# The last seven of 79 expert blocks behind a condition, and half a shared-expert batch moved to the end

## The chip, the cores and the metric

The kernel runs on one core of a Trainium2 chip. The metric is the device time of one execution in microseconds, where lower is better; a kernel's time is the median of several runs. The engines that matter here are TensorE (PE, matmuls; PEld is its weight load), VectorE (DVE), ScalarE (ACT), GpSimd (POOL) and SyncE (SP, which issues most DMAs). Each engine works through its own list of instructions in order, and waits for the others through semaphores.

## The reference: what is computed

One transformer block on four batches of 512 tokens of width 256, in fp32. A modulation from a small conditioning input scales and shifts two layer norms and gates two residuals. The first half is causal attention with 32 heads of width 8. The second half is a mixture of experts, cut here to its core:

```python
x = x + ga * attention(h)
h = layernorm(x) * (1 + cb) + sb
cw = combine_weights(h, gate_w)             # [T, 16]: four experts a token, the others 0
for e in range(16):
    a = swiglu(h @ expert_up_w[e].T)        # 256 -> 2 x 176
    out = out + cw[:, e:e+1] * (a @ expert_down_w[e].T)
out = out + swiglu(h @ shared_up_w.T) @ shared_down_w.T   # the shared expert, 2 x 352
x = x + gb * out
```

Which experts a token takes is known only at run time: of four groups of four experts the two with the greatest score are kept, and of these the four best experts.

## The kernel before, in words

**Routing.** After the attention of each batch, its normalized rows (256 values, the token's number and 16 weights) are scattered by POOL into `rows_d`, a table in HBM with a stretch of rows for each expert. VectorE counts how many rows each expert has (`upto`). `make_table` (L318) works out, from those counts, a list of blocks of 128 rows: `last` holds a running count of the blocks begun, and `row` and `of` hold, one partition a block, the first row of a block and its expert. 2048 tokens x 4 experts are 64 full blocks, and each of 16 experts may leave one begun block, so `NBLK` = 64 + 15 = 79 blocks always suffice. Blocks that are not begun read a row stretch that is blank, and add zeros to a row of the accumulator that nobody reads.

**Experts.** In `ffn` (L1501) each block `j` goes through `block(j)` (L1550): SP reads the block's row into a register and fetches x (`fetch`, L1560), TensorE transposes it (`pt`, L1571), ACT copies it (`xt`), TensorE multiplies with the expert's up weights (`pu`, L1591), ACT and VectorE form the gated product (`sg_b` L1601, `a_b` L1605), TensorE transposes it back (`pb`, L1610), VectorE copies it (`at_b`, L1614), TensorE multiplies with the down weights (`py`, L1619), ACT weighs the rows (`y_b`, L1629), and POOL scatters them with an add into an accumulator in HBM (`put`, L1632). There are two accumulators by turns, and a third from block 63 (`LAST`) on; a scatter waits until the one before it on the same accumulator has landed.

**Shared expert.** `shared(b, ...)` (L398) works on half batches of 256 tokens: three chunks of up matmuls (L417), tanh on ACT (L428), two products on VectorE (L436, L437), two outputs of down matmuls (L455), a gating on VectorE (L465) and an add into `x_sb` on POOL (L471). All eight halves are planned ahead of the blocks; the last runs between the first blocks.

**Ends.** The rows of an expert are ordered by batch, so the first batches are complete before all blocks are done. `end(b, n, due)` (L1674) loads the two accumulators' rows of batch b with SP (L1687), and adds, gates and adds the residual on VectorE (L1693, L1696, L1701), in two halves, then stores (L1704). It is planned at block n + 14, with n = 31, 47 and 63 for the first three batches. Its operations on VectorE also wait, in the plan, for the copies (`backs`) of later blocks, one each, so that they are spread over them. The fourth batch is finished after the last block (L1728 to L1739): twelve loads by SP and ACT, then adds on POOL and VectorE, and four stores.

**Order.** On TensorE, VectorE, ACT and SP the order is the kernel's own: `Plan` (L85) takes operations with a cost, needs, a due time and buffers that they take and give back, and issues at each step the one that can start first. It works with the estimates written beside the operations; once issued, an engine's order is fixed. POOL's order is left to the framework's scheduler, apart from some links.

## Time and profile before

| what | value |
|---|---|
| median of 3 runs (lowest, highest) | 724.9 us (723.86, 727.31) |
| the profiled execution's own time | 723.11 us |
| its span, first to last instruction | 721.4 us |
| mean granted TensorE clock | 0.962 |
| PE busy | 648.1 us (90%) |
| DVE, ACT, POOL busy | 441.5, 314.7, 360.3 us |
| 316 records of pu (L1591) | 106.6 us, 460 ns each |
| 316 records of py (L1619) | 81.4 us, 379 ns each |
| 79 scatters put (L1632) | 128.0 us, 1621 ns each |

Records of TensorE overlap: a matmul's record lasts longer than the distance to the next one, so time on TensorE is read from the starts. The profile tells the 40 equal slices of the span as digits, tenths of busy time. The expert blocks fill about the last third of the span.

### The profile page before, as it was taken

The page shows a single profiled execution, that of the slowest core. Times are in us where ns is not written, and L with a number is a line of the kernel's source. Part 1 is how long each engine was busy: PE and PEld are TensorE (multiplying, and loading weights), DVE is VectorE, ACT ScalarE, POOL GpSimd, SP SyncE. Part 2 cuts the span into 40 slices and gives each one's busy share as a digit, 9 for nine tenths or more (in the row PEclk, how much of TensorE's full clock was granted, in tenths as well). Part 3 has the DMA queues.
Part 4 walks back from the last instruction along what each step waited for, and adds up shares of the span by engine and source line. Part 5 has one row for each costly group of instructions (what it writes and reads, how often), then busy time and mean ns, then how long its engine had stood idle before and what let it go on. Part 6 is the DMA issues. An engine that isn't in the chain of part 4 may idle for free.

```text
span 721.4 us, 12934 instructions
## 1 busy us (share of the span) xinstructions
PE 648.1 (90%) x4188; PEld 401.3 (56%) x4188; DVE 441.5 (61%) x1206; ACT 314.7 (44%) x551; POOL 360.3 (50%) x454
## 2 busy tenths in 40 slices
PE   4778899999999999999998798799999999999980
PEld 3343344454544545445453277588777777777750
DVE  4568678889888788887977035644333334444343
ACT  1313455664556645555655511013344444444430
POOL 7401233336277453664727625552566666666682
PEclk9789999999999999999999879899999999999995
DMA  5351161212234232554201178851467678777765
GB/s 167 80 130 26 42 170 45 53 41 69 61 111 118 78 98 68 161 164 126 65 4 60 44 225 232 209 143 33 81 109 108 110 110 180 128 160 139 148 88 132
DMA packets 58002, 77.81 MB, mean 108 GB/s; under 512 B 8620, under 2 KB 50316, under 8 KB 56784
## 3 DMA queue, kind: packets, MB, share of 16 engines
q1 hardware_dynamic: 42714, 56.96, 28.6%
q0 software_dynamic: 14448, 19.31, 16.6%
q10 hardware_dynamic: 774, 0.72, 0.4%
q8 instruction: 34, 0.56, 0.3%
q14 instruction: 32, 0.26, 0.1%
HBM read 43.73 MB, written 32.83 MB: 106 GB/s over the span
## 4 chain that ended last, share of the span: by engine, by line
PE 66%; DVE 19%; DMA 5%; issue 4%; ACT 2%; POOL 2%; SPq 0%; ACTq 0%; DVEq 0%; POOLq 0%
PE pu L1591 13%; PE py L1619 10%; PE pa L1012 9%; PE pr L899 8%; DVE mx_s L920 7%; PE p L1042 7%; PE pu L417 4%; PE py L455 3%; PE pr L907 2%; PE pb L1610 2%; PE pt L1571 2%; DMA qx<-mrow 2%; ACT ex L1054 2%; DVE xn L654 2%; DMA kx<-kd 1%
## 5 line engine op out<-in xcount | busy, mean ns | idle before, releaser
L920 DVE TENSOR_REDUCE mx_s<-pr 128x1 f32<-128x384 f32 (+3 forms) x352 | 212.5, 635 | 39.3 <-PE pr L907 35.9
L1054 ACT ACTIVATE ex<-p 128x1024 f32<-128x1024 f32 (+1 forms) x192 | 162.5, 882 | 105.7 <-PE p L1042 97.6
L1061 POOL TENSOR_SCALAR_AFFINE_SELECT ex<-ex 128x256 f32<-128x256 f32 (+1 forms) x192 | 93.1, 491 | 193.8 <-ACT ex L1054 192.4
L1632 POOL DMA_INDIRECT acc_d<-y_b,token x79 | 128.0, 1621 | 77.2 <-DVE token L1584 26.3
L899 PE MATMUL pr<-kx,qx 125*128 125x384 bf16 (+3 forms) x512 | 122.8, 304 | 12.6 <-DVE mx_s L920 9.7
L1591 PE MATMUL pu<-up_sb,xt 128*128 x316 | 106.6, 460 | 0.0
L1042 PE MATMUL p<-qx,kx 128*128 128x256 bf16 (+3 forms) x512 | 97.5, 302 | 7.3 <-DMA qx<-mrow 4.4
L1012 PE MATMUL pa<-ex,vaug 128*32 128x512 f32 (+3 forms) x1024 | 96.6, 448 | 2.2 <-POOL ex L1061 2.1
L907 PE MATMUL pr<-seen,ident_h 128*128 128x128 bf16 (+2 forms) x352 | 86.7, 246 | 0.0
L899 PEld LDWEIGHTS <-qx 125*128 125x128 bf16 x512 | 46.6, 99 | 67.5 <-issue 48.7
L1619 PE MATMUL py<-down_sb,at_b 88*128 x316 | 81.4, 379 | 1.2 <-DVE at_b L1614 1.2
L1605 DVE TENSOR_TENSOR a_b<-sg_b,pu 128x176 f32<-128x176 f32 x79 | 26.6, 337 | 80.2 <-ACT sg_b L1601 80.2
L1383 POOL DMA_INDIRECT rows_d<-row,slot x64 | 62.7, 979 | 25.1 <-DVE slot L1380 12.6
L1619 PEld LDWEIGHTS py<-down_sb,at_b 88*128 88x128 f32 x316 | 59.7, 189 | 22.1 <-ACT y_b L1629 1.7
L1591 PEld LDWEIGHTS pu<-up_sb,xt 128*128 128x128 f32 x316 | 53.9, 190 | 16.8
L1042 PEld LDWEIGHTS <-kx 128*128 128x128 bf16 x512 | 41.0, 98 | 39.6 <-issue 23.7
L1629 ACT ACTIVATE y_b<-py,cw_b 128x256 f32<-128x256 f32 x79 | 37.5, 474 | 46.1 <-PE py L1619 46.1
L1614 DVE COPY at_b<-pb 88x256 f32<-88x256 f32 x79 | 33.2, 420 | 36.0 <-PE pb L1610 36.0
L1601 ACT ACTIVATE sg_b<-pu 128x176 f32<-128x176 f32 x79 | 25.1, 318 | 59.9 <-PE pu L1591 59.8
L417 PE MATMUL pu<-h2t,sup_sb 128*128 128x256 f32 (+1 forms) x192 | 47.7, 402 | 1.7 <-DVE a L437 1.7
L907 PEld LDWEIGHTS <-ident_h 128*128 128x128 bf16 x352 | 34.5, 98 | 25.7 <-issue 19.6
L1012 PEld LDWEIGHTS pa<-ex,vaug 128*32 128x32 f32 x1024 | 21.6, 108 | 36.5 <-issue 20.2
(184 smaller groups left out, 730.7 us busy)
## 6 DMA issues: line engine op xcount, KB each, us to landing
x<-rows_d SPq DMA_DIRECT2D x79, 136.5 KB
qx<-qd SPq DMA_DIRECT2D x48, 192.0 KB
up_sb<-in_up_t SPq DMA_DIRECT2D x8, 704.0 KB
acc_d<-blank SPq DMA_DIRECT2D x18, 256.0 KB
qd<-pt SPq DMA_DIRECT2D x16, 192.0 KB
s<-acc_d SPq DMA_DIRECT2D x12, 256.0 KB
down_sb<-in_down_t SPq DMA_DIRECT2D x8, 352.0 KB
rows_d<-blank SPq DMA_DIRECT2D x17, 136.5 KB
```

Of the source, the lines that this page charges most:

```text
L417: nc.tensor.matmul(st["p"][:rows, w, :], lhsT=sup_sb[:, k, c0 : c0 + rows], rhs=h2t[:, k, c1 : c1 + half], start=(k == 0), stop=(k == KC - 1),
L899: nc.tensor.matmul(pr[:, h, :], lhsT=qx[s % 3][:QKZ, REP * j + r + h, ts(i, P)], rhs=kx[s % 3][:QKZ, j, :w], start=True, stop=False, skip_ ...
L907: nc.tensor.matmul(pr[:, :, w - P :], lhsT=ident_h, rhs=seen.unsqueeze(1).to_broadcast([P, n, P]), start=False, stop=True, skip_group_chec ...
L920: nc.vector.tensor_reduce(mx[s][:, i, c0 : c0 + n], st["pr"], AX.X, ALU.max)
L1012: nc.tensor.matmul(st["pa"][32 * r : 32 * r + 32, c * P :], lhsT=vaugs[b % 2][:, c, SLOTS * n + j, :], rhs=exs[r], start=(j == 0 and c == ...
L1042: nc.tensor.matmul(pe[:, h, :], lhsT=kx[s % 3][:, j, ts(c, P)], rhs=qx[s % 3][:, REP * j + r + h, c * P :], start=True, stop=True,)
L1054: nc.scalar.activation(ex, st["pe"], AF.Exp, scale=qk_scale)
L1061: nc.gpsimd.affine_select(out=st["ex"][:, :, 0:P], in_=st["ex"][:, :, 0:P], pattern=[[0, n], [1, P]], base=0, channel_multiplier=-1, compa ...
L1383: dma = nc.gpsimd.indirect_dma_start(out=rows_d, out_offset=bass.IndirectOffsetOnAxis(ap=st["slot"][:, i, k : k + 1], axis=0), in_=st["row ...
L1591: nc.tensor.matmul(st["pu"], lhsT=st["xt"][:, k, :], rhs=up_sb[:, bass.ds(st["e"], 1), k, :].rearrange("p e f -> p (e f)"), start=(k == 0) ...
L1619: nc.tensor.matmul(st["py"], lhsT=st["at"][:, c, :], rhs=down_sb[:, bass.ds(st["e"], 1), c, :].rearrange("p e d -> p (e d)"), start=(c == ...
L1632: dma = nc.gpsimd.indirect_dma_start(out=acc_d[j % (2 if j < LAST else 3)], out_offset=bass.IndirectOffsetOnAxis(ap=st["token"][:, 0:1], a ...
```

## The change

A constant `SURE` = 72 splits the blocks. Blocks 0 to 71 are issued as before. The table also gives the number of blocks begun, as an integer. After the 72 blocks, every engine loads that number into a register, and blocks 72 to 78 stand in a part that runs only if it is over 72. What follows the conditional part is the end of the fourth batch, as before.

The second half of the last batch's shared expert is no longer planned ahead of the blocks. It is planned after block 71, with a late due time, and may start only once the up matmuls of block 71 are issued.

The end of the third batch is planned at block 71 in place of block 77, since no later block is sure. The list of copies that its VectorE operations wait for is filled up with None, which stands for no wait.

```diff
+SURE = 72
...
         def rows():
...
+            last = t["last"]
...
-            for name in ("row", "of"):
+            t["all"] = last[:, B * E - 1 :]
+            for name in ("row", "of", "all"):
                 t[f"{name}_i"] = pool.tile([P, 1], mybir.dt.int32, name=f"{name}_i", bufs=1)
                 nc.vector.tensor_copy(t[f"{name}_i"], t[name])
...
-    def shared(b, due, up_bank, down_bank, first=None):
+    def shared(b, due, up_bank, down_bank, first=None, halves=(0, 1)):
...
-        for n in range(2):
+        for n in halves:
             unit(n)
...
-            shared(b, due, up_bank, down_bank)
+            shared(b, due, up_bank, down_bank, halves=(0, 1) if b < B - 1 else (0,))
...
                 "PE", 1.28, up, [xt, weights], due, takes=[h["pu"]], gives=[h["xt"]]
             )
+            ups.append(u)
...
-        backs = []
+        backs, ups = [], []
...
-            pace = iter(backs[n + 8 :])
+            pace = iter(backs[n + 8 :] + [None] * 6)
...
-        for j in range(NBLK):
+        for j in range(SURE):
             puts.append(block(j))
             for b in range(B - 1):
                 n = (b + 1) * S * TOPK // P + E - 1
-                if j == n + 14:
+                if j == min(n + 14, SURE - 1):
                     end(b, n, 300.0 + n)
+        shared(B - 1, lambda: 1000.0, up_bank, down_bank, ups[-1], halves=(1,))
         plan.go()
+        many = nc.values_load(
+            t["all_i"][0:1, 0:1], min_val=0, max_val=NBLK,
+            skip_runtime_bounds_check_because="counted above",
+        )
+        with tc.If(many > SURE):
+            for j in range(SURE, NBLK):
+                puts.append(block(j))
+            plan.go()
```

## The prediction

> **What bounds the kernel now.** I read the page first, then the chain that ended last, then the busy time by stretches, then the engines' timelines where the change lands.
>
> The page, its span line and three of its rows of 40 slices (18 us each):
>
> ```profile
> span 721.4 us, 12934 instructions
> ...
> PE   4778899999999999999998798799999999999980
> ...
> PEclk9789999999999999999999879899999999999995
> DMA  5351161212234232554201178851467678777765
> ```
>
> TensorE is full in nearly every slice, also from slice 27 on (486 us), where the expert blocks run. Its clock is full there.
>
> The busy time by stretches; columns are each engine's busy us (instructions), granted clock, DMA share, GB/s:
>
> ```profile
> core 0: us, PE busy (x) PEld busy (x) DVE busy (x) ACT busy (x) POOL busy (x), PEclk, DMA share, GB/s
> 453.80:457.20 3.40, 3.37 (x10) 2.50 (x11) 2.89 (x18) 0.38 (x1) 1.79 (x2) 0.63 0.33 112
> 540.00:600.00 60.00, 60.00 (x291) 45.62 (x290) 21.58 (x97) 28.00 (x73) 37.18 (x25) 1.00 0.71 114
> 600.00:690.00 90.00, 90.00 (x436) 68.38 (x435) 41.03 (x160) 41.91 (x109) 57.98 (x36) 1.00 0.77 147
> ```
>
> From 540 to 690 us TensorE never rests; VectorE and ScalarE are busy less than half of it. The chain that ended last, near its end (start, us, who):
>
> ```profile
> 690.40 1.19 PE pu L1591 x4
> 692.89 1.19 PE pu L1591 x4
> 695.16 1.19 PE pu L1591 x4
> 698.04 1.10 PE py L1619 x4
> 699.96 1.12 PE py L1619 x4
> 702.28 1.27 issue
> 703.55 4.97 DMA acc_d<-y_b,token
> 709.45 1.97 DMA s<-acc_d
> ```
>
> One block costs 692.89 - 690.40 = 2.49 us. The last scatter is issued at 703.55 and lands 4.97 us later; the last batch is then loaded, summed and stored. From the first load that waits for it (SP's timeline, 708.59) to the end of the span are 12.8 us.
>
> **The change part by part.** I place the new instructions by their order on each engine, and give them times from this trace.
>
> *The seven blocks.* Counting the reference's choices on its own inputs, every expert gets between 483 and 576 tokens, five of them more than 512: 11 x 4 + 5 x 5 = 69 blocks are begun. So the condition (over 72) is false and blocks 72 to 78 do not run: 7 x 2.49 = 17.4 us of a TensorE-bound stage.
>
> *The half batch that leaves the first blocks.* It has three chunks of 8 TensorE records (1.73 us from start to start of two groups in TensorE's timeline) and two outputs of 6 records (1.30 us): 3 x 1.73 + 2 x 1.30 = 7.8 us. TensorE has no gap from 495 us on, so all blocks begin 7.8 us earlier. Its new neighbours hide nothing of it: x of the first blocks is fetched from 478 us on, and a block's pu reaches its transposed product in 0.9 us while 1.4 us of other matmuls stand between. Its two adds on POOL (0.73 each) stood in the 0.9 us that POOL idles between scatters. It comes back at the end, below.
>
> *The adds of the third batch lose their pace.* This is the costly part. The function end adds 3 VectorE operations for each half batch. For the third batch they are now planned at block 71 instead of 77. Before, each waited in the plan for the copy of another block (71 and on). Now only one of the six has such a block left; for the others None is given. In the new VectorE order the three operations of the second half stand right behind the product of block 69, ahead of the copy of block 68. What they wait for:
>
> ```profile
> SPq L1687 <- DMA acc_d<-y_b,token: 14.2, 4, 5.8
> ```
> ```profile
> 674.68 3.50 SPq L1687 DMA_DIRECT2D s<-acc_d  x4
> ```
> ```profile
> 682.75 0.42 DVE L1614 COPY at_b<-pb 88x256 f32<-88x256 f32 x1 [0.40 <-PE pb L1610]
> 683.09 0.68 DVE L1693 TENSOR_TENSOR s<-s,s 128x512 f32<-128x512 f32 x1
> ```
>
> The first is the waits of SP's queue (us in total, times, longest), the others timelines. The four loads of the third batch wait for the scatters of blocks 63 and 64 (issued 670.89 and 672.75 in POOL's timeline, landed 674.7 and 676.6) and are issued from 674.68 on. By the trace's completion records the last two land at 681.4 and 683.0. Today the add comes at 683.09, in time. Everything moved 7.8 us earlier, the loads land at about 675.2. But VectorE now comes to the add much sooner: the pu of block 76 starts at 690.24, so that of block 69 at 690.24 - 7 x 2.49 = 672.8, less 7.8 = 665.0; its product ends 2.1 us later (as in 692.73 to 694.80), at 667.1. **VectorE waits 8.1 us**, in order. Behind it stand the copy of block 68, the products of 70 and 71 and all of the last blocks; TensorE can still do the pu of 70 and 71, to 669.9. Scatters lag their blocks by 5.3 us at block 63 (3.3 at 62), since 62 and 63 write the same accumulator; this lag moves with the DMA traffic, so I hold the landing possible from 672.5 to 677.5.
>
> After the landing: three operations of 0.68, the copy 0.42 and 0.1 to 0.2 of handing over: the py of block 68 starts at 677.7.
>
> *The last sure blocks and the half batch.* From there TensorE has 4 x 0.87 (py) + 3 x 0.22 (pb) + 7.8 (half batch) = 11.9 us, and waits about 1.1 us: the last chunk's tanh and two products take 1.6 us (ACT L428 0.38, DVE L436 and L437 0.42 each, handing over), of which the first two down matmuls cover 0.87, and one copy comes late by 0.3. The scatter of block 71 lands meanwhile: its y is ready 7.7 us after 677.7, so it lands about 690.
>
> *The clock.* TensorE stands still from 669.9 to 677.7. In the stretch table, 453.80 to 457.20 has a clock of 0.63; its matmuls are
>
> ```profile
> 453.83 2.92 PE L417 MATMUL pu<-h2t,sup_sb 128*96 128x256 f32 x8 [1.72 <-DVE a L437]
> 456.54 1.81 PE L455 MATMUL py<-sdown_sb,a 128*128 128x256 f32 x4
> ```
>
> after pauses of 2.31 and 1.72 us: 12 records in 4.5 us, which at full clock are 2.6. The Trainium skill ("TensorE: Matmul & The Clock Gate", why this matters for your kernels) says the same against this change: no TensorE pause over some 3 us, since one idle window halves the clock. By the row the restart costs 1.9 us, by the page half of a 3.4 us window, 1.7; I take 1.8. With a warm clock it would be 0. So TensorE ends at 677.7 + 13.0 + 1.8 = 692.5.
>
> *The branch.* Each engine loads the count, compares, jumps, and raises its semaphores for the blocks left out. SP's loads now wait for TensorE and for POOL to have done so. SP and ACT get there early, hidden by the half batch. POOL comes last: its add (0.73) ends with TensorE, then a register load (0.28 to 0.36 in the L390 rows), the jump and some ten semaphore steps of 0.04: about 1.4 us. A taken jump is not in the trace. The Trainium skill ("Runtime: NRT & Kernel Launch", instruction fetch mechanics) warns that a target outside the fetched window stalls for a fetch. The nearest rows: instruction packets take 1.1 us, a small load lands in 2.1. From below 0, since the part left out is only some 60 to 90 instructions for each engine; from above two fetches, 4.2. I take 0.7: nearer to the lower end, because the fetch runs ahead of so short a jump. Loads start at 692.5 + 1.4 + 0.7 = 694.6.
>
> *The end.* 12.8 us as today, and 0.5 since ACT's four loads, which today are issued at 703.6 and land before SP's, now share the DMA engines with them. The added copy of the count (about 0.06) and the second add on POOL behind the branch (0.73) lie beside waits for DMA; uncovered they would cost just that.
>
> **Sum**: 694.6 + 12.8 + 0.5 = 707.9 against a span of 721.4: 13.5 us less (removed 17.4; the wait and the cold clock take most of what the filled drain would have added). The profiled execution itself took 723.1 and would take 709.6; the median of the runs shown is 724.9, which gives 711.4. I predict **711**.
>
> **The rivals.**
> *No wait on the adds* (the loads land before 667, because the lag of the scatters vanishes). For: the lag was 0.28 us up to block 35. Against: loads for the first batches raise it each time (landing of a scatter 3.8 to 5 us). Then py of 68 starts at 669.9, TensorE ends at 682.9, loads start at 685, end at 698.3: 23.1 us less, 702.
> *The jump is dear* (two fetches or more on each engine, or other costs of a conditional part): 3.5 to 8 us above my sum, 715 to 719.
> *The conditional part runs, and the change does nothing but add* (slower): price: the blocks start after a full drain at 693.5, the last pu is at 694.4 + 6 x 2.49 = 709.3, its scatter is issued 8.55 later (703.55 - 695.00), lands 5 later, and the end takes 12.9: 735.7, 14 more, 739. It decides from a count of 73 on; the count of 69 speaks against it.
>
> **How the numbers follow.** The likeliest case 0.75 (its own range 706.5 to 715), no or little wait 0.12, a dear jump 0.08, slower 0.05. The range for 8 in 10: 703 to 716. A change under 0.5% (3.6 us) can't be told from none: faster 0.91, same 0.04, slower 0.05; the likeliest and the first two rivals are all faster.
>
> **What would show it.** Right: 72 scatters on POOL instead of 79; the block spacing still 2.49; block starts 7.8 us earlier; VectorE idle some 8 us ahead of the add (new line 1697), released by a DMA; TensorE idle just after; a clock near 0.5 in the next 3 us; the first load of the last batch near 694. Wrong: no idle time ahead of the add; a gap of several us between TensorE's end and that load; 79 scatters.

## The result and the profile after

| | before | after |
|---|---|---|
| median (lowest, highest), 4 runs each on one chip | 726.11 us (723.86, 727.64) | 714.74 us (712.89, 716.5) |
| ratio, 95% interval | | 0.9845 [0.9805, 0.9886] |
| profiled execution, its span | 723.11, 721.4 us | 716.5, 714.7 us |
| mean granted TensorE clock | 0.962 | 0.946 |

The changed kernel is faster by 11.4 us (8 to 14). 711 was predicted, with a range of 703 to 716; 714.7 lies near its upper end (1.2 of the 3.7 us between them come from the kernel before, whose median was 724.9 when the prediction was made and is 726.1 here). The sum of the prediction was a span of 707.9; the profiled span is 6.8 us longer. Where these 6.8 us are is the subject of what follows.

From the page of the kernel after: the span line, and the rows of TensorE and its clock in 40 slices of 17.9 us.

```profile
span 714.7 us, 12633 instructions
...
PE   4687999999999999999999779699999999999780
...
PEclk9768999999999999999999789889999999999976
```

TensorE is still full through the block stage, but the third slice from the end has a 7 where it had a 9, and the clock has a 7 in the slice behind it, where it had a 9.

The same place by stretches, kernel after (columns as in the prediction: us, then busy us of PE, PEld, DVE, ACT and POOL with instructions, granted clock, DMA share, GB/s).

```profile
600.00:671.00 71.00, 71.00 (x344) 53.94 (x343) 31.93 (x127) 32.92 (x85) 43.31 (x29) 1.00 0.71 127
674.00:677.90 3.90, 0.00 (x0) 0.00 (x0) 0.00 (x0) 0.21 (x1) 1.47 (x1) 1.00 0.93 227
677.90:681.70 3.80, 0.00 (x0) 0.00 (x0) 2.40 (x5) 0.00 (x0) 0.00 (x0) 0.50 0.17 35
681.70:688.10 6.40, 6.34 (x17) 4.95 (x18) 1.04 (x6) 0.86 (x2) 1.55 (x1) 0.50 0.31 63
688.20:698.00 9.80, 9.22 (x42) 7.01 (x41) 5.62 (x12) 2.10 (x5) 5.86 (x4) 1.00 0.46 69
```

TensorE never rests up to 671 us. Its last matmuls end at 673.85, then it does nothing for 7.9 us, then works 6.4 us at half clock, and only then at full clock.

Who stopped it: VectorE's timeline of the kernel after (start, us, engine, line, operation; in brackets the idle time before it and who ended that).

```profile
670.57 0.34 DVE L1608 TENSOR_TENSOR a_b<-sg_b,pu 128x176 f32<-128x176 f32 x1 [1.21 <-ACT sg_b L1604]
679.16 0.69 DVE L1697 TENSOR_TENSOR s<-s,s 128x512 f32<-128x512 f32 x1 [8.26 <-DMA s<-acc_d]
...
681.30 0.41 DVE L1617 COPY at_b<-pb 88x256 f32<-88x256 f32 x1
```

This is the wait of the prediction, in the predicted order: product of block 69, then the third batch's add for 8.26 us, then the copy of block 68. The four loads it needs are in SP's timeline, with the last batch's loads below them.

```profile
670.28 3.40 SPq L1691 DMA_DIRECT2D s<-acc_d  x4
...
700.08 4.48 SPq L1746 DMA_DIRECT2D s<-acc_d  x8
```

By the completion records the four land at 673.7, 676.9, 678.3 and 679.0. TensorE's timeline of the kernel after:

```profile
671.32 2.53 PE L1594 MATMUL pu<-up_sb,xt 128*128 x8
681.76 2.08 PE L1622 MATMUL py<-down_sb,at_b 88*128 x4 [7.91 <-DVE at_b L1617]
683.63 0.63 PE L1613 MATMUL pb<-ident,a_b 128*88 128x128 f32 x2
684.06 1.91 PE L420 MATMUL pu<-h2t,sup_sb 128*128 128x256 f32 x4
...
688.89 1.03 PE L1622 MATMUL py<-down_sb,at_b 88*128 x4
...
695.93 2.00 PE L458 MATMUL py<-sdown_sb,a 96*128 96x256 f32 x8 [0.51 <-DVE a L440]
```

The first py after the pause takes 2.08 us, the one at 688.89 takes 1.03: the clock. TensorE ends at 697.93. The end of the chain that ended last, kernel after:

```profile
690.71 9.23 DMA acc_d<-y_b,token
700.95 2.98 DMA s<-acc_d
```

The chain puts all of 690.71 to 699.94 down to a scatter. By the completion records that scatter (block 70's) landed at 695.0 and block 71's, the last, at 697.0; what the loads waited for from there on is the branch (see e5_no_branch).

**A measure without the start's noise.** Single profiles of one and the same program differ by several us long before the change: in the profiles of the kernels below, the first pu of the block stage starts anywhere from 494.6 to 510.8 us, although the code up to there is the same but for the half batch and one copy of the count. Much of this is between chips: 494.6 to 496.2 in the four profiles of e5 and e7 to e9, which share a chip, and 502.3 to 510.8 in the seven of the two other chips. Those seven lose 8.6 to 10.8 us against the kernel before at one place, between 466 and 471 us of its time; what TensorE waits for there on these chips is not settled.

The two profiles of the first comparison can be laid side by side too, since TensorE's records are the same in both up to 495 us. The kernel after is 2.3 us late at 39 us already and 2.5 at 446 us, far ahead of the change. Another 1.4 come between 446 and 466 us (of the kernel before's time), where it spends two steps of 3.4 us at half clock (462.87 to 469.70) and the kernel before one (461.52 to 464.93). Together these make the 3.9 us of a late start that the account below needs.

From the first pu to the pu of block 70, however, every kernel without the half batch ahead shows 172.30 us, and every one with it 178.4 (e6_taken aside, whose block 70 stands behind the condition). So I measure the tail: from the start of block 70's pu (by the records of pu, four a block) to TensorE's end, to the last batch's loads on SP, and to the end of the span. For the kernel before the tail is 46.1 us, with seven more blocks in it; the prediction's sum amounts to 40.4 for the kernel after.

| kernel | to TensorE's end | to the loads | to the end | saved, by the tail | ratio to the kernel before | saved, by the ratio |
|---|---|---|---|---|---|---|
| before | 25.8 | 33.3 | 46.1 | | 1 | |
| predicted | 25.0 | 27.1 | 40.4 | 13.5 | | |
| after | 26.6 | 28.8 | 43.4 | 10.5 | 0.9845 | 11.3 |
| e7_after_again | 27.7 | 29.8 | 44.3 | 9.6 | 0.9879 | 8.7 |
| e1_paced | 19.0 | 21.2 | 35.6 | 18.3 | 0.9764 | 17.3 |
| e2_warm | 23.2 | 25.4 | 40.0 | 13.9 | 0.9860 | 10.3 |
| e3_cond_only | 22.2 | 26.0 | 41.8 | 4.3 | 0.9950 | 3.7 |
| e4_half_only | 32.6 | 32.3 | 45.6 | 8.3 | 0.9920 | 5.9 |
| e5_no_branch | 27.8 | 27.4 | 41.2 | 12.7 | 0.9837 | 11.8 |
| e8_spread | 15.5 | 18.5 | 33.1 | 20.8 | 0.9725 | 19.9 |
| e8_spread_again | 15.5 | 18.4 | 33.4 | 20.5 | 0.9723 | 20.3 |
| e9_spread_pairs | 15.5 | 18.4 | 34.2 | 19.7 | 0.9741 | 18.7 |
| e10_early_branch | 16.0 | 17.8 | 32.1 | 21.8 | 0.9671 | 24.1 |

"Saved, by the tail" is 46.1 less the tail, and 7.8 more where the half batch no longer stands ahead of the blocks (6.12 of them lie between the two pu, and one chunk, 1.73, just ahead of the first pu: 495.15 to 496.88 in the kernel before). "By the ratio" is one less the ratio, times the median of the kernel before on that chip (726.1 for the first comparison, 733.6 for e1 to e4, 721.9 for e5 and e7 to e9, 733.6 for e6, e8_spread_again and e10). The ratios have intervals of 0.003 to 0.004 to each side, 2 to 3 us. In e5 SP's first load is issued early, at 23.1; its others follow from 27.4 on.

The two columns of savings agree within 1.5 us in all but e2, e4 and e10, where they differ by 2 to 4. So the tail of one profile tells about what the medians tell, and it can be taken apart into steps.

### The profile page after: what moved, and what is told of

It reads as the page before. It is cut to its first block, busy times and chain, and to the rows that moved or that the text cites. A ratio compares the mean times of both kernels' runs of the same rounds, so it can differ in the third digit from the quotient of the medians.

```text
span 714.7 us, 12633 instructions
## 1 busy us (share of the span) xinstructions
PE 638.6 (89%) x4104; PEld 391.3 (55%) x4104; DVE 435.7 (61%) x1179; ACT 307.1 (43%) x530; POOL 344.3 (48%) x447
## 3 DMA queue, kind: packets, MB, share of 16 engines
q0 software_dynamic: 13440, 18.39, 15.8%
## 4 chain that ended last, share of the span: by engine, by line
PE 62%; DVE 16%; DMA 10%; issue 5%; ACT 3%; POOL 1%; SPq 1%; ACTq 0%; DVEq 0%; POOLq 0%
PE pu L1594 12%; PE pa L1015 9%; PE py L1622 8%; PE pr L902 8%; DVE mx_s L923 7%; PE p L1045 7%; DMA down_sb<-in_down_t 4%; PE pu L420 3%; PE pr L910 3%; PE pt L1574 2%; PE pb L1613 2%; ACT ex L1057 2%; PE py L458 2%; DMA qx<-mrow 2%; DMA qx<-qd 1%
## 5 line engine op out<-in xcount | busy, mean ns | idle before, releaser
L1635 POOL DMA_INDIRECT acc_d<-y_b,token x72 | 112.5, 1562 | 81.6 <-DVE token L1587 26.6
L902 PE MATMUL pr<-kx,qx 125*128 125x384 bf16 (+3 forms) x512 | 124.2, 307 | 11.8 <-DVE mx_s L923 8.9
L1594 PE MATMUL pu<-up_sb,xt 128*128 x288 | 97.0, 460 | 0.0
L1622 PE MATMUL py<-down_sb,at_b 88*128 x288 | 76.0, 386 | 7.9 <-DVE at_b L1617 7.9
L1386 POOL DMA_INDIRECT rows_d<-row,slot x64 | 62.6, 979 | 25.1 <-DVE slot L1383 12.6
L1622 PEld LDWEIGHTS py<-down_sb,at_b 88*128 88x128 f32 x288 | 55.5, 193 | 27.6 <-DVE at_b L1617 8.5
L1608 DVE TENSOR_TENSOR a_b<-sg_b,pu 128x176 f32<-128x176 f32 x72 | 24.2, 337 | 75.7 <-ACT sg_b L1604 75.7
L1594 PEld LDWEIGHTS pu<-up_sb,xt 128*128 128x128 f32 x288 | 49.2, 190 | 15.5
L1632 ACT ACTIVATE y_b<-py,cw_b 128x256 f32<-128x256 f32 x72 | 34.2, 475 | 52.4 <-PE py L1622 52.4
L1617 DVE COPY at_b<-pb 88x256 f32<-88x256 f32 x72 | 30.3, 420 | 33.0 <-PE pb L1613 33.0
L910 PEld LDWEIGHTS <-ident_h 128*128 128x128 bf16 x352 | 34.8, 99 | 24.7 <-issue 18.5
L1604 ACT ACTIVATE sg_b<-pu 128x176 f32<-128x176 f32 x72 | 22.9, 318 | 56.9 <-PE pu L1594 56.1
L420 PEld LDWEIGHTS pu<-h2t,sup_sb 128*128 128x128 f32 (+1 forms) x192 | 37.7, 201 | 9.8 <-DVE a L440 2.0
```

The source lines that it names most:

```text
L420: nc.tensor.matmul(st["p"][:rows, w, :], lhsT=sup_sb[:, k, c0 : c0 + rows], rhs=h2t[:, k, c1 : c1 + half], start=(k == 0), stop=(k == KC - 1),
L902: nc.tensor.matmul(pr[:, h, :], lhsT=qx[s % 3][:QKZ, REP * j + r + h, ts(i, P)], rhs=kx[s % 3][:QKZ, j, :w], start=True, stop=False, skip_ ...
L910: nc.tensor.matmul(pr[:, :, w - P :], lhsT=ident_h, rhs=seen.unsqueeze(1).to_broadcast([P, n, P]), start=False, stop=True, skip_group_chec ...
L1386: dma = nc.gpsimd.indirect_dma_start(out=rows_d, out_offset=bass.IndirectOffsetOnAxis(ap=st["slot"][:, i, k : k + 1], axis=0), in_=st["row ...
L1594: nc.tensor.matmul(st["pu"], lhsT=st["xt"][:, k, :], rhs=up_sb[:, bass.ds(st["e"], 1), k, :].rearrange("p e f -> p (e f)"), start=(k == 0) ...
L1622: nc.tensor.matmul(st["py"], lhsT=st["at"][:, c, :], rhs=down_sb[:, bass.ds(st["e"], 1), c, :].rearrange("p e d -> p (e d)"), start=(c == ...
```

## The experiments

Line numbers in the lines of a variant are the variant's own, some lines off those of the kernel after. The diffs are against the kernel after.

**e1_paced: is it the unpaced adds?** All six operations of the third batch's end wait in the plan for the copy of block 71, and so stand behind every copy.

```diff
-            pace = iter(backs[n + 8 :] + [None] * 6)
+            pace = iter(backs[n + 8 :] + [backs[-1]] * 6)
```

> The changed kernel, with the six adds of the third batch waiting in the plan for the copy of block 71, so that no block's operation stands behind them on VectorE. Theory (VectorE's wait of 8.3 us for the loads, and the slow restart of TensorE after it, are what the change pays): the pause of TensorE before the py of block 68 goes, TensorE ends some 9 us earlier, and the time falls by 8 to 10 us against the changed kernel, to about 705. Rival (the last scatters and their landing set the end, the wait lies beside them): TensorE's pause goes but the time moves by less than 3 us, 712 to 715.

Measured: 717.94 us (711.95 to 718.75), ratio 0.9764 [0.9722, 0.9806]. TensorE's timeline of e1_paced:

```profile
676.90 1.35 PE L1594 MATMUL pu<-up_sb,xt 128*128 x4
678.09 1.03 PE L1622 MATMUL py<-down_sb,at_b 88*128 x4
...
688.30 1.97 PE L420 MATMUL pu<-h2t,sup_sb 128*96 128x256 f32 x8 [3.56 <-DVE a L440]
```

And VectorE's, of the same kernel:

```profile
682.22 0.69 DVE L1697 TENSOR_TENSOR s<-s,s 128x512 f32<-128x512 f32 x1 [0.48 <-DMA s<-acc_d]
684.32 0.69 DVE L1697 TENSOR_TENSOR s<-s,s 128x512 f32<-128x512 f32 x1 [1.40 <-DMA s<-acc_d]
...
687.38 0.41 DVE L439 SCALAR_TENSOR_TENSOR t<-t,pu 128x256 f32<-128x256 f32 x1
```

No pause and no slow clock between the blocks' end and the half batch: the tail is 7.8 us shorter than the first profile of the kernel after (8.7 than the second). The unpaced adds in front of the copies are therefore the cause of the pause, and the pause with its clock costs at least these 8 us, since a new wait is already taken off them: the adds have only been moved to the next bad place. They now stand in front of the shared expert's first product, at 687.38; its bank of PSUM is needed for the third chunk, and TensorE waits 3.56 us for it.

**e2_warm: what does the clock cost?** Sixteen matmuls without use (32 records) fill TensorE's pause behind the pu of block 71.

```diff
+        def warm():
+            w = ps1.tile([P, 2, D], F32, name="p1")
+            for _ in range(16):
+                nc.tensor.matmul(w[:, 0, :], lhsT=h2t[:, 0, 0:P], rhs=h2t[:, 0, 0:D], start=True, stop=True)
+        plan.add("PE", 0.0, warm, [ups[-1]], 0.0)
```

> The changed kernel, with 16 added matmuls on TensorE behind the pu of block 71 (about 6.9 us into a bank that nobody reads), inside the pause of 7.9 us. Theory (the restart is slow because the clock fell in the pause, 3.1 us lost): py of block 68 takes 1.03 again in place of 2.08, and the time falls by 2 to 3 us, to about 712. Rival (the restart is slow for want of data from VectorE and ScalarE): the rows after the pause stay as slow and the time stays within 1 us of 714.7.

Measured: 724.17 us (721.27 to 725.16), ratio 0.9860 [0.983, 0.989]. TensorE's timeline of e2_warm:

```profile
684.10 7.07 PE L1731 MATMUL p<-h2t 128*128 128x256 f32 x32
691.93 1.13 PE L1622 MATMUL py<-down_sb,at_b 88*128 x4 [0.76 <-DVE at_b L1617]
```

VectorE still waits 8.02 us for the loads, but all that follows on TensorE runs at full speed: from the first py to TensorE's end 13.04 us, against 16.17 in the kernel after (681.76 to 697.93). 13.0 was the prediction's figure for a warm clock. So the restart cost 3.1 us in the first profile, not 1.8. The tail is 3.4 us shorter than in the kernel after. The ratio, 0.9860, lies between the two of the kernel after (0.9845 and 0.9879) and can't show 3 us; this experiment speaks through its profile alone.

**e3_cond_only: the condition without the half batch.** Both halves of the last shared batch run ahead of the blocks, as before the change.

```diff
-            shared(b, due, up_bank, down_bank, halves=(0, 1) if b < B - 1 else (0,))
+            shared(b, due, up_bank, down_bank)
...
-        shared(B - 1, lambda: 1000.0, up_bank, down_bank, ups[-1], halves=(1,))
```

> The condition alone: the last half batch of the shared expert runs before the blocks as it did before the change. Theory (the wait of 8 us stays, since adds and loads both come 7.8 us later, and with it the half batch at the end fills time that is lost anyway): about 717, that is 9 us under before, though 17.4 us of blocks are gone. Rival A (the blocks come off whole): 709. Rival B (the half batch's 7.8 us are the larger part of the gain): 722.

Measured: 730.32 us (728.99 to 731.66), ratio 0.995 [0.9923, 0.9977]: 3.7 us of the 17.4 that the seven blocks were, and not the 9 of the theory. The saving is that of rival B (722 against 726). TensorE's timeline of e3_cond_only:

```profile
696.42 2.08 PE L1622 MATMUL py<-down_sb,at_b 88*128 x4 [8.47 <-DVE at_b L1617]
...
699.44 2.08 PE L1622 MATMUL py<-down_sb,at_b 88*128 x4 [0.51 <-DVE at_b L1617]
```

And its last stretch:

```profile
695.00:709.00 14.00, 9.52 (x22) 5.88 (x22) 5.19 (x13) 1.89 (x4) 5.78 (x4) 0.50 0.30 47
```

The pause is the same, but now only the drain of four blocks follows it, with a gap in each block. TensorE never gets its clock back: 0.50 to the end, and the four py come 3.0 to 3.1 us apart. Its steps of 3.41 us are 82 to 85% busy there, none is full. The loads start 3.8 us after TensorE's end and the span ends 15.8 us after them.

**e4_half_only: the half batch without the condition.** All 79 blocks run; the half batch follows block 78.

```diff
-        for j in range(SURE):
+        for j in range(NBLK):
...
-                if j == min(n + 14, SURE - 1):
+                if j == n + 14:
...
-        many = nc.values_load(...)
-        with tc.If(many > SURE):
-            for j in range(SURE, NBLK):
-                puts.append(block(j))
-            plan.go()
```

> The moved half batch alone: all 79 blocks run without a condition, and the half batch follows block 78. Theory (7.8 us leave a full TensorE and come back beside the 7 us in which the last scatter waits and lands): TensorE ends near where it ended, the last scatter lands some 7 us earlier, about 719, 7 us under before. Rival (TensorE's end, later than the scatter's landing, takes the gain back): 724 or more.

Measured: 728.12 us (727.46 to 728.82), ratio 0.992 [0.9897, 0.9944]. TensorE's timeline of e4_half_only:

```profile
705.77 3.62 PE L420 MATMUL pu<-h2t,sup_sb 128*128 128x256 f32 x16
709.23 1.03 PE L458 MATMUL py<-sdown_sb,a 128*128 128x256 f32 x4
710.76 2.00 PE L458 MATMUL py<-sdown_sb,a 96*128 96x256 f32 x8 [0.51 <-DVE a L440]
```

With its adds paced the half batch runs in the holes of the drain and at full clock; its 7.8 us vanish nearly whole (8.3 by the tail, 5.9 by the ratio). Condition alone 4.3 and half batch alone 8.3 by the tail make 12.6 together; the whole change gives 10.5 and 9.6. By the ratios 3.7 and 5.9 make 9.6, against 11.3 and 8.7. So the two parts nearly add up, and the half batch is the larger one, as rival B of e3 had it. The pause on the adds is in the condition alone as well, so it does not explain the 2 to 3 us that are missing by the tail; these stay open.

**e7_after_again: the kernel after, a second time,** as the reference for the three below, which ran in the same rounds.

> The changed kernel itself, unaltered, on the chip of the three runs below and in their rounds, so that each of them can be set against it and not only against the kernel before. Expected of it: a ratio to the kernel before of 0.980 to 0.989 (0.9845 on the chip of the first comparison); TensorE's end to the last batch's first loads 2.0 to 2.3 us, those loads to the end of the span 14 to 15 us, VectorE's wait on the third batch's adds 7.5 to 9 us. If the 3.9 us by which its first profile began the block stage late belong to that one execution and not to the kernel, its median here lies below what that profile's sum gives, at a ratio of 0.980 to 0.983; if they belong to the kernel, at 0.984 to 0.987.

Measured: 713.79 us (710.1 to 715.81), ratio 0.9879 [0.9845, 0.9913]. That is above both spans expected, though its interval takes in most of the upper one, so the medians don't decide whether the first profile's late start belonged to it alone. Its own first pu starts at 496.2, 2.9 us earlier than in the first profile, but on another chip, where the kernel before is 4.3 us faster too (721.9 against 726.1 us), so this comparison does not decide it either; the records up to 446 us, above, do for 2.5 us of the 3.9. The tail is no shorter. VectorE's and TensorE's waits are longer here:

```profile
678.60 0.69 DVE L1697 TENSOR_TENSOR s<-s,s 128x512 f32<-128x512 f32 x1 [10.55 <-DMA s<-acc_d]
```

and the stretches around it, in e7_after_again:

```profile
671.00:674.80 3.80, 0.00 (x0) 0.00 (x0) 0.00 (x0) 0.32 (x1) 3.19 (x3) 1.00 0.85 182
675.00:681.10 6.10, 0.00 (x0) 0.00 (x0) 2.37 (x5) 0.00 (x0) 0.00 (x0) 0.50 0.52 115
681.20:685.10 3.90, 3.90 (x10) 3.11 (x11) 0.97 (x5) 0.47 (x1) 1.04 (x1) 0.50 0.20 69
```

The longer pause (10.2 us) has a shorter slow stretch behind it, 3.9 us against 6.4. In both profiles the half clock lasts 10.24 us, three steps of 3.41, which is the grid on which the clock changes in these records. I laid TensorE's busy records on that grid:

```
kernel after                        e7_after_again
from us  busy   clock               from us  busy   clock
671.09    81%   1.0                 668.08    86%   1.0
674.50     0%   1.0                 671.49     0%   1.0
677.91     0%   0.5                 674.90     0%   0.5
681.33    87%   0.5                 678.32    16%   0.5
684.74   100%   0.5                 681.73   100%   0.5
688.15   100%   1.0                 685.14   100%   1.0
```

A step without work halves the clock of the next one; the clock comes back, here, only behind a step that was full. A restart in the middle of a step is thus charged the rest of that step and the whole of the next. Only if it comes so early that the step is still nearly full (over 89% busy always sufficed in these traces, 87% here did not) does the clock return at the step's end. That makes some 3.0 to 6.4 us at half speed, a loss of 1.5 to 3.2 (an estimate from this grid). The two profiles have 6.4 / 2 = 3.2 and 3.9 / 2 = 2.0.

**e5_no_branch: what does the skipped condition cost?** The count is not loaded, there is no condition, and the code of blocks 72 to 78 is left out.

```diff
-        many = nc.values_load(...)
-        with tc.If(many > SURE):
-            ...
```

> The changed kernel without the read of the number of blocks begun, without the condition and without the code of blocks 72 to 78, which it leaves out altogether (for these inputs they hold nothing). What it gains on the changed kernel is what the conditional costs where it is skipped. My theory: 2.15 us lie between TensorE's end and the last batch's first loads in the changed kernel, and without the condition the loads wait only for the last scatter-side work and issue about 0.5 us after TensorE's end, so 1.5 to 1.8 us less; GpSimd's semaphore instruction of 1.0 us between its branch and its next work goes away with the branch. Rival: the loads wait for something else at that point (the shared expert's last add on GpSimd, or scatters that have not landed), and then it gains under 0.5 us. Second rival: code of the skipped part costs the engines time that the profile shows nowhere, and it gains 3 us or more. End of loads to end of span stays 14 to 15 us if the shared completion semaphores make it, and falls to 13 us if the branch makes it.

Measured: 709.98 us (707.11 to 711.91), ratio 0.9837 [0.9807, 0.9868], 3.8 us under the kernel after by the medians and 3.1 by the tail, about twice what was expected. SP's timeline of e5_no_branch:

```profile
690.02 8.39 SPq L1738 DMA_DIRECT2D s<-acc_d  x8
```

TensorE ends at 694.67. By SP's records one load is issued at 690.02 already, the second at 694.28, when block 71's scatter has landed (issued 689.79, landed 694.26), 0.4 us ahead of TensorE's end; ScalarE's four go out between, from 692.65 on. From 694.28 to the end are 13.8 us instead of 14.5, with five of the twelve loads out before. Without the condition the loads wait for scatters only. With it they wait for GpSimd to pass the branch, and GpSimd comes late, since one of the shared expert's two adds, whose input comes from TensorE's last group of down matmuls but one, stands in front of the branch. GpSimd's timeline of the kernel after, with the branch between the two adds:

```profile
697.18 0.72 POOL L474 TENSOR_TENSOR x_sb<-x_sb,o 128x256 f32<-128x256 f32 x1 [2.58 <-DVE o L468]
700.08 0.72 POOL L474 TENSOR_TENSOR x_sb<-x_sb,o 128x256 f32<-128x256 f32 x1 [2.18 <-DMA acc_d<-y_b,token]
```

The second add's wait is put down to a scatter, but the last one had landed at 697.0. The records of the kernel after name the pieces between TensorE's end (697.93) and the loads (700.08): the load of the count on GpSimd takes 0.50 us, the branch itself 0.06 there and 0.05 to 0.24 on the others, the next instruction follows 0.1 to 0.5 us after it, and one instruction of GpSimd that raises the counts of the skipped scatters' semaphore takes 1.0 us (698.98 to 699.99). SP's first load is issued at 700.08, right behind it. Block 71's scatter had landed at 697.0, so without the branch the loads could have gone 3 us earlier: the number of the second rival, but in plain sight of the profile and not beside it.

**e8_spread: the adds where VectorE has room.** The six operations are planned behind the shared expert's products, two behind each.

```diff
-    def shared(b, due, up_bank, down_bank, first=None, halves=(0, 1)):
+    def shared(b, due, up_bank, down_bank, first=None, halves=(0, 1), prods=None):
...
+                if prods is not None:
+                    prods.extend([last, last])
...
-            pace = iter(backs[n + 8 :] + [None] * 6)
+            pace = iter(prods or backs[n + 8 :])
...
-            for b in range(B - 1):
+            for b in range(B - 2):
...
-                if j == min(n + 14, SURE - 1):
+                if j == n + 14:
...
-        shared(B - 1, lambda: 1000.0, up_bank, down_bank, ups[-1], halves=(1,))
+        shared(B - 1, lambda: 1000.0, up_bank, down_bank, ups[-1], halves=(1,), prods=prods)
+        n = (B - 1) * S * TOPK // P + E - 1
+        end(B - 2, n, 300.0 + n, prods)
```

> The changed kernel with the third batch's six VectorE operations placed by name: the first two behind the shared expert's first product, the next two behind its second, the last two behind its third, two at a time in the gaps that VectorE has there. In the changed kernel they stood in front of the copies of blocks 68 to 71 and waited 8.3 us for their loads; in the paced variant they no longer waited there but stood all together in front of the products, and TensorE's third chunk waited 3.6 us. My theory: both waits go. TensorE runs blocks 68 to 71 and the half batch without a pause over 1 us, its end is 7 to 9 us earlier relative to the start of the block stage than in the changed kernel (about 190.5 instead of 198.9 us after the first block's product), the time is 6 to 9 us less than the changed kernel's, and 2 to 4 us less than the paced variant's, ratio to the kernel before 0.972 to 0.977. Rival: VectorE is what limits the half batch, and two operations of 0.69 us between two products delay the bank that TensorE needs next as much as six at once; then a wait of 1 to 1.5 us appears at each of the second and third chunks and the gain on the changed kernel is under 5 us. Second rival: TensorE's pause and its slow clock were not what set the end, and the gain is under 2 us.

Measured: 702.23 us (699.75 to 704.13), ratio 0.9725 [0.9695, 0.9756]: 11.6 us under the kernel after by the medians, 10.3 to 11.2 by the tails, more than the 6 to 9 expected. TensorE's timeline of e8_spread:

```profile
676.42 3.62 PE L420 MATMUL pu<-h2t,sup_sb 128*128 128x256 f32 x16
679.88 1.03 PE L460 MATMUL py<-sdown_sb,a 128*128 128x256 f32 x4
681.74 2.00 PE L460 MATMUL py<-sdown_sb,a 96*128 96x256 f32 x8 [0.84 <-DVE a L440]
```

The longest wait left is 0.84 us, and the clock stays full. TensorE ends 15.5 us after block 70's pu. The rival of the prediction that had no wait on the adds comes to 682.9 - 667.45 = 15.45 by its own numbers. The loads, at 686.71, start 2.97 us after TensorE's end, later than in the kernel after: GpSimd's load of the count took 0.80 us here and its semaphore steps began later.

**e9_spread_pairs: fewer, larger loads at the end.** The spread variant, the last batch's sums loaded in 6 transfers of two tiles. Against e8_spread:

```diff
-        for n in range((B - 1) * NT, B * NT):
-            three = [ep.tile([P, D], F32, name=f"s{n}_{i}") for i in range(3)]
+        for n in range((B - 1) * NT, B * NT, 2):
+            three = [ep.tile([P, 2, D], F32, name=f"s{n}_{i}") for i in range(3)]
             for t, acc, eng in zip(three, acc_d, (nc.sync, nc.scalar, nc.sync)):
-                eng.dma_start(out=t, in_=acc[ts(n, P), :])
-            sums.append(three)
+                eng.dma_start(out=t, in_=acc[n * P : (n + 2) * P, :].rearrange("(n p) d -> p n d", p=P))
+            sums += [[t[:, i, :] for t in three] for i in range(2)]
```

> The spread variant with the last batch's sums loaded in 6 transfers of two tiles each instead of 12 of one tile, so that no transfer needs a completion semaphore that another still holds. The additions and the stores stay one tile each. My theory: the fifth load on SP waited 1.4 us in the changed kernel for a semaphore shared with the first load of ScalarE's queue; without the wait the first loads to the end of the span fall from 14.6 to 12.5 to 13.5 us, 1 to 2 us less than the spread variant. Rival: a load of two tiles lands later than one of one tile, all four tiles start later, and this costs more than the semaphore did: first loads to end 14.5 to 16 us, the time equal to or up to 1.5 us above the spread variant.

Measured: 701.94 us (700.46 to 708.7), ratio 0.9741 [0.9701, 0.9781]: no difference from e8_spread. SP's timeline of e9_spread_pairs, and below it GpSimd's:

```profile
685.76 1.91 SPq L1750 DMA_DIRECT2D s<-acc_d  x4
```
```profile
691.36 1.40 POOL L1753 TENSOR_TENSOR s<-s,s 128x256 f32<-128x256 f32 x2 [4.88 <-DMA s<-acc_d]
```

The four loads are issued in a row. In the kernel after the fifth stood 1.4 us behind the fourth, 1.0 of it waiting for a completion semaphore that an earlier load still held. But the first add starts 5.6 us after the first load, against 4.0 in e8_spread (690.74 after 686.71), and the end is 15.8 us after the loads instead of 14.6, as the rival had it (14.5 to 16). My theory falls: the wait for the semaphore was there, but taking it away did not shorten the end.

**e10_early_branch: the condition in another place.** The spread variant; the plan is carried out up to block 71's scatter and the shared expert's third product, then comes the condition, then the rest of the half batch. Against e8_spread:

```diff
-        plan.go()
+        plan.go(until=[puts[-1], prods[-1]])
+        kept = plan.open, plan.left, dict(plan.free)
+        plan.open, plan.left = {engine: [] for engine in plan.LAG}, 0
...
         with tc.If(many > SURE):
             for j in range(SURE, NBLK):
                 puts.append(block(j))
             plan.go()
+        plan.open, plan.left, plan.free = kept
+        plan.go()
```

> The spread variant with the condition moved ahead of the last of the half batch: every engine branches as soon as block 71's scatter and the shared expert's third product are handed out, and the two down products, the two gates, two of the third batch's six operations and GpSimd's two adds come behind the branch. In the spread variant the loads of the last batch started 2.97 us after TensorE's end, because GpSimd reached the branch only behind the first gate's add and then spent 1.0 us in one semaphore instruction that SP waits for; in the changed kernel without the condition they had resumed 0.4 us ahead of TensorE's end, when block 71's scatter had landed. My theory: the price of the skipped condition is its place on GpSimd's queue, so the loads now start when the last scatter has landed, 0 to 0.6 us after TensorE's end, and the time falls by 2 to 3 us against the spread variant, ratio to the kernel before 0.968 to 0.971. Rival: TensorE's own branch, between the third chunk and its down products, takes 0.7 us and more on the path, or the loads are held by another engine's part of the branch; then the gain is under 1 us, or the time is longer.

> The spread variant unaltered, on the chip of the run above and in its rounds, to set the earlier branch against. Expected: ratio to the kernel before 0.970 to 0.976, TensorE without a pause over 1 us from block 68 on, the first load of the last batch 2.8 to 3.1 us after TensorE's end, 14 to 15 us from there to the end of the span.

Measured: 711.41 us (706.6 to 716.88), ratio 0.9671 [0.964, 0.9703]; the spread variant in the same rounds 714.06 us (713.26 to 714.33), ratio 0.9723 [0.9699, 0.9746]. The intervals overlap by a hair; by the medians the earlier branch gains 2.7 us, by the tail 1.3. TensorE's, SP's and GpSimd's timelines of e10_early_branch:

```profile
696.18 2.86 PE L460 MATMUL py<-sdown_sb,a 128*128 128x256 f32 x12 [1.29 <-ACTq L1740]
```
```profile
700.89 5.84 SPq L1754 DMA_DIRECT2D s<-acc_d  x8
```
```profile
696.83 1.55 POOL L1637 DMA_INDIRECT acc_d<-y_b,token  x1 [0.30 <-issue]
```

TensorE pays for its own branch (16.0 us to its end instead of 15.5), and the loads start 1.85 us after that end instead of 2.97. Two things end just ahead of them: block 71's scatter, issued late in this profile, at 696.83, lands at 700.70, and GpSimd's step of 1.0 us, which starts when block 70's has landed, ends at 700.80. So the loads are no longer held by the shared expert's adds, but the profile doesn't tell which of these two holds them. This is the fastest kernel of the study against the kernel before, with e8_spread close behind. What the condition costs is shown by e5; how much of that its place makes, and how much this variant recovers, is less sure.

**e6_taken: the condition holds.** SURE at 68.

```diff
-SURE = 72
+SURE = 68
```

> The changed kernel with SURE at 68 instead of 72: for these inputs 69 blocks are begun, so the condition holds and the last eleven blocks, 68 to 78, run inside the conditional part. This prices my slower rival, the conditional part that runs. The rival's sum was 14 us above the kernel before for seven blocks inside; with eleven the work is the same and the stop between the two parts comes four blocks earlier. Expected: 79 scatters, one pause of TensorE of 2 to 5 us between the half batch and the first block inside, the blocks inside at 2.49 us again, a last scatter 8 to 9 us after the last block's product, and a time 12 to 20 us above the kernel before (ratio 1.017 to 1.028). If the blocks' own code inside the conditional part is slower (fetches of code at each iteration's start, cold clock), the spacing inside is over 2.6 us and the ratio above 1.03. If the condition costs nothing when it holds, the ratio is 0.99 to 1.005.

Measured: 745.99 us (743.98 to 747.93), ratio 1.0153 [1.0119, 1.0186]: 11.2 us above the kernel before by the ratio, just under the span expected, and 12.4 by the medians, just inside it. TensorE's timeline of e6_taken:

```profile
691.74 4.63 PE L458 MATMUL py<-sdown_sb,a 128*128 128x256 f32 x10 [10.58 <-DVE a L440]
...
697.26 1.59 PE L1594 MATMUL pu<-up_sb,xt 128*128 x4
```

All 79 scatters are there, and inside the condition the blocks come 2.49 us apart again (711.54, 714.03, 716.52), so the code there is no slower. The pause is not between the half batch and the first block inside, where it was expected: the branch lies hidden there. It is inside the half batch, 10.58 us, since in this order the third batch's adds stand in front of the shared expert's last two products. The slower rival was real in kind and near its price (14 us), and 69 blocks begun are what kept it away. That count belongs to these inputs. With the reference's inputs drawn from five other seeds, the blocks begun are 73, 74, 71, 73 and 73: for four of the five the condition would hold, and if e6_taken is a guide, the change would then cost time.

## Why the prediction was right, and where its sum was off

The time and the sign are right, and so is the mechanism: each of its steps is in the profile. Its span of 707.9 became 714.7. Point by point:

- **Seven blocks.** Right: 72 scatters, block starts 663.85, 666.34, 668.83, 671.32 in TensorE's records, 2.49 apart.
- **The half batch ahead.** Right as to the work: from the first pu to block 70's pu 178.42 us became 172.30, and the rest of the 7.8 lies ahead of the first pu. But the block stage should have begun at 495.15 and began at 499.02. Of these 3.9 us, 2.5 are there at 446 us, where the two kernels don't differ yet, and the rest fits one more step at half clock by 466 us. So they belong to the execution and not to the step: the prediction carried one profile's start into another execution as if it were fixed. The medians agree: the profiled execution before was 3.0 us under its kernel's median, the one after 1.8 over.
- **The wait on the adds.** Right, and nearly to the figure: 8.1 predicted, 8.26 and 10.55 measured. The order on VectorE and the loads as the releaser are as described. The size hangs on when the scatters of blocks 63 and 64 land; the prediction's span for the landing of the loads, of 5 us, just covers both profiles.
- **The clock.** Mechanism right, size off: 1.8 predicted, 3.1 and about 2 measured. The prediction took one window of 3.4 us, from a row whose pauses were short and from the page "TensorE: Matmul & The Clock Gate". The same page (Part 1) calls that window free-running, and the grid above shows what follows: the part of a window in which work returns comes, in most positions, on top of a full one. So 1.8 was near the least that the grid allows (1.5 to 3.2), and its middle, about 2.3, would have been the better term. Nor was a pause of over some 3 us enough by itself to halve the clock: e1_paced's of 3.56 us did not.
- **TensorE's end.** With these two 26.6 and 27.7 us after block 70's pu, where 25.0 were predicted: 1.6 and 2.7 of the difference.
- **The branch.** The sum of 2.1 us was measured as 2.15, by luck in its parts. Its 1.4 us hold GpSimd's add of 0.73 behind TensorE's end, though its words have the add end with TensorE, and so it was (697.90 and 697.93). The register load took 0.50 us and not about 0.3. The fetch that it allowed 0.7 us for does not show: the instruction after the branch comes within 0.5 us on each engine. In their place GpSimd spends 1.0 us in one semaphore step. What the prediction didn't see is that the loads need not have waited for TensorE's end: without the condition they start before it (e5), and the whole of the condition is worth 3.1 us, not 2.1.
- **The end.** The term that was mis-sized by most that holds in both profiles: 13.3 predicted, 14.6 and 14.5 measured. Before, ScalarE's four had landed (706.2 to 708.7) as SP's eight began; those eight were all in 6.1 us later. Now all twelve are issued from 700.0 on and are in after 7.0 us, the first after 2.8 us instead of 2.1. The prediction gave this overlap 0.5 us. The first load to the last store's issue takes 11.5 us instead of 10.2, and what follows the last store 3.1 instead of 2.6. The other runs fit: where some of ScalarE's loads went out 1.6 us and more ahead of most of SP's (e4, e5, e6), the end took 12.9 to 13.8 us, where all began together 14.3 and more. No run varies this alone.

The loads of this last point, on ScalarE and SP in the kernel before, and on ScalarE in the kernel after (SP's there, from 700.08 on, are shown above):

```profile
703.62 1.79 ACTq L1732 DMA_DIRECT2D s<-acc_d  x4
708.59 3.92 SPq L1732 DMA_DIRECT2D s<-acc_d  x8
```
```profile
699.99 1.84 ACTq L1746 DMA_DIRECT2D s<-acc_d  x4
```

In sum: 3.9 (start) + 1.6 (TensorE) + 0.05 (branch) + 1.3 (end) = 6.8. On medians the start's 3.9 fall away for the most part, and the saving is 11.3 and 8.7 us instead of 13.5.

Of the rivals, the dear jump is refuted: no fetch shows, though the condition costs 3.1 us in all. The rival without a wait did not happen in this kernel, but e8_spread shows that it had TensorE's part right, its end to 0.1 us, and the price nearly: 20 us saved where it gave 23.1. The change as made leaves half of that gain on the table, in the place of six VectorE operations.

Of the 25.2 us that were taken out of the stretch ahead (17.4 and 7.8), about 10 were saved. By the difference of tails to e8_spread, 10 to 11 went into the wait on the adds with its clock, and by e5_no_branch 3 into the condition. The 1 to 2 us left are not settled.

## What to carry to other kernels

When a list of operations that paced others is shortened, look at what stood behind each of them in the in-order engine: a wait that was harmless at its old place stops the engine at its new one, and putting all of them at the end of the line (e1) only moves the wait to the next consumer. Place them in gaps by name, and then read the order and the waits again. A condition that is skipped still costs something: what it needs from each engine comes only when that engine has worked through its queue, so look which one passes it last, and try it where that one passes early (e10 did, for a gain of 1 to 3 us that is not quite clear of the noise). And compare profiles from a common mark inside the program, not from their starts.

## What the runs showed of the hardware

- The clock is decided on a grid of 3.41 us, and not by the same rule in both directions. Over all thirteen profiles, from 390 us on: at full clock a step under 40% busy always halved the next one and a step over 55% never did (between, both occur: 41% without, 54% with). At half clock a step under 80% never brought it back and one over 89% always did (between, both occur). So e1_paced's pause of 3.56 us, split over two steps that were 45 and 51% busy, cost no clock, while e3_cond_only's drain, with gaps of 0.5 to 0.6 us, stayed cold to its end.
- The skipped part of seven blocks (12633 instructions run in place of 12934) showed no fetch of code: branch 0.05 to 0.36 us, next instruction within 0.5 us, in the nine profiles that skip it. GpSimd's step that makes up for its skipped scatters took 1.0 us in each of them.
- The mark-to-mark time of the block stage, 172.30 us over 70 blocks, was the same to 0.01 us in ten profiles of different chips, while the start of that stage varied by 16 us between chips and by 1.6 us in the four profiles of one chip.
